# Rows of attention maxima: from TensorE products with the identity to a VectorE block transpose and a trip through DRAM

## The chip, the cores and the metric

The kernel runs on one core of a Trainium2 chip. The metric is the time of one execution on the device in microseconds (us), and the figure quoted for a kernel is the median of several executions. Profiles are single executions with the hardware profiler on. The engines are called as in the profile: PE (TensorE, with PEld for its weight loads), DVE (VectorE), ACT (ScalarE), POOL (GpSimd) and SP (SyncE, which here only issues transfers).

## The reference, cut to what matters

One layer: attention over 4096 tokens of width 256 with 16 heads of width 16, then a residual and a layer norm, then a gated feed-forward part with hidden width 1024, a second residual and a second layer norm. The change lies in the attention:

```python
proj = quant4(x) @ ternary_weight(Wqkv_w).T + Wqkv_b
q = proj.reshape(B, N, h, dk).transpose(0, 2, 1, 3)
k = proj.reshape(B, h, N, dk)
v = proj.reshape(B, h, N, dk)
q, k = (rotary(q, N), rotary(k, N))
ql, kl = (q @ U, k @ U)
att = jnp.einsum('bhnr,bhmr->bhnm', ql, kl) / math.sqrt(dk)
y = jax.nn.softmax(att, axis=-1) @ v
...
return quant4(y) @ ternary_weight(Wo_w).T
```

The softmax needs the largest score of every query and head. The kernel computes all scores twice: once with queries on the partitions, to find the maxima, and once with keys on the partitions, to make the weights, with the maximum subtracted inside the product.

## The kernel before, in words

**Units and steps.** The attention is cut into 64 units (`NU`): 8 pairs of heads times 8 blocks of 512 queries (`QB`). A unit `u` has 32 steps (`NKT`), so there are 2048 steps. Each step of the main loop at line 690 can do three things, all for different places of the stream:

- `largest(s)`: two score products (L463, one for each head `j` of the pair, each over 64 rows) into two PSUM tiles of the pool `ps_1`, which has three buffers, and one DVE reduction to a maximum for each (L471). At the last step of a unit, DVE reduces the 8 partial maxima of each query and head to one (L476), rounds it to the matmul type (L483) and keeps the rest of the rounding as a second part (L484). The two parts go into columns 0, 1 and 64, 65 of `m_aug`, a 128 x 128 tile for each of the four query tiles, otherwise zero.
- `weights(s - LAG)`: four products (L504) into one tile `sc`: first minus ones times the rows of maxima, `mrows[u]`, which starts each sum with the negated maximum, then keys times queries. ACT then takes the exponential of 128 x 1024 values (L512).
- `values`: once in two steps, eight products of the weights with the values (L526) into the tile `av`.

**The rows of maxima.** The maxima come out of `largest` with a query on each partition, and `weights` needs them as rows along the free dimension. `largest_rows(u)` does that: four products of `m_aug` with the identity (L491) into one `ps_1` tile, and an ACT copy of it to `mrow` in SBUF (L495). It is put at step 32(u+1)+2, that is two steps after the unit's last maxima, and the unit's first `weights` follow at step 32u+LAG, with `LAG` = 36, two steps later still.

**Order.** Nothing is scheduled by a planner. `at(step, f)` puts a piece of work at a step; at each step, first that list runs, then `largest` (odd steps) or `weights`, then the other. Every engine takes its instructions in that written order. Apart from the three streams the list holds the making of queries (L426, L434) and keys (L356 to L395), the projection of later blocks of x, the end of a unit (`finish`, L541 to L565, at the steps `base + NKT + AVLAG - 1` and `+ 3`, with `base` = 32u + `LAG`), the comparison of weights with their rounded copies (L582 to L590, one chunk every second unit, its DVE reduction at step 30 of a unit), and weight loads near the end. SP issues the x and weight-check loads (L626, L582) and the writes of a unit's output to `y_dram` (L565), also in written order.

**Start and end.** In steps 0 to 35 only `largest` runs, and after step 2047 only `weights` and `values` run, for `LAG` steps and a few more. Then the feed-forward part follows (`ffn`), PE-bound and untouched by the change; its first block's preparation, `start_front`, is put at the fixed steps 2050 to 2070.

Of the kernel before, what the change touches and what calls it, by code (L numbers as in the profile page):

```python
# [9 lines left out]
F32 = mybir.dt.float32  # L10
F32R = mybir.dt.float32r
# [3 lines left out]
ALU = mybir.AluOpType  # L15
AX = mybir.AxisListType
PSUM = bass.MemoryType.PSUM

P = 128
# [6 lines left out]
QB = 512  # L26
NQB = N // QB
NKT = N // P
DH = 1024
NC = DH // P  # L30
BT = 4
# [6 lines left out]
def attn_ffn_kernel(  # L38
# [22 lines left out]
    nc = tc.nc  # L61
# [4 lines left out]
    stat = ctx.enter_context(tc.tile_pool(name="stat", bufs=4))  # L66
# [6 lines left out]
    identr = const.tile([P, P], F32R, name="identr")  # L73
# [6 lines left out]
    dram = ctx.enter_context(tc.tile_pool(name="dram", bufs=1, space=bass.MemoryType.DRAM))  # L80
# [157 lines left out]
    with ExitStack() as actx:  # L238
        big = actx.enter_context(tc.tile_pool(name="big", bufs=1))
# [11 lines left out]
        gmat = big.tile([P, P], F32, name="gmat")  # L251
        minus = big.tile([P, P], F32R, name="minus")

        m_aug = [big.tile([P, BT, P], F32R, name=f"m_aug{i}") for i in range(2)]

        qpool = actx.enter_context(tc.tile_pool(name="qpool", bufs=2))
        ppool = actx.enter_context(tc.tile_pool(name="ppool", bufs=8))
# [2 lines left out]
        ps_1 = actx.enter_context(tc.tile_pool(name="ps_1", bufs=3, space=PSUM))  # L260

        def bank1(shape, dt):
            return ps_1.tile(shape, dt, name="ps1")

        def set_up():

            nc.sync.dma_start(out=x_bufs[0], in_=x_t[:, ts(0, BT), :])
            tw = [ppool.tile([P, 2, D], F32, name=f"tw{i}", tag="pr") for i in range(2)]
            wabs = ppool.tile([P, 2, 2, D], F32, name="tabs", tag="pr")
            neg = ppool.tile([P, 2, 2, D], F32, name="tneg", tag="pr")  # L270
            nc.sync.dma_start(out=tw[0], in_=wqkvT.rearrange("(k p) o -> p k o", p=P))
            small = ppool.tile([P, 2 * QB], F32, name="small", tag="pr")
            ut, ut8, mask = small[:32, :DK], small[:32, P : 2 * P], small[:, 2 * P : 3 * P]
            nc.sync.dma_start(out=ut, in_=uT)
            nc.sync.dma_start(out=mask, in_=blockmask)
            tables = ((cos, cos_q, cos_k), (sin, sin_q, sin_k))
            for src, _, tk in tables:
                nc.sync.dma_start(out=tk, in_=src.rearrange("(a p c) f -> p a c f", a=2, p=P))
            nc.sync.dma_start(out=bias_bc, in_=bqkv.partition_broadcast(P))
            for src, tq, _ in tables:  # L280
                nc.sync.dma_start(out=tq, in_=src.rearrange("(t p) f -> p t f", p=P))
            nc.sync.dma_start(out=x_bufs[1], in_=x_t[:, ts(1, BT), :])
            nc.sync.dma_start(out=tw[1], in_=woT.rearrange("(k p) o -> p k o", p=P))

            ternary(tw[0], wabs[:, 0], neg[:, 0], bank1, sgn_qkv, alpha_qkv)
            nc.gpsimd.tensor_copy(
                ut8.rearrange("r (j e) -> r j e", e=DK), ut.unsqueeze(1).broadcast_to([32, 8, DK])
            )
            psg = bank1([P, 512], F32)
            nc.tensor.matmul(psg[:, :P], lhsT=ut8, rhs=ut8, start=True, stop=True)  # L290
            nc.vector.tensor_tensor(gmat, psg[:, :P], mask, ALU.mult)

            def later():

                nc.gpsimd.memset(minus.bitcast(F32), -1.0)
                for i in range(2):
                    nc.gpsimd.memset(m_aug[i].bitcast(F32), 0.0)
                nc.gpsimd.memset(v_chunk[:, :, :, DK : DK + 1], 1.0)
                nc.gpsimd.memset(v_all[:, :, H * (DK + 1) :], 0.0)
                ternary(tw[1], wabs[:, 1], neg[:, 1], bank1, sgn_o, alpha_o)  # L300

            return later
# [140 lines left out]
            return natural, transposed  # L443

        NU = (H // 2) * NQB
        LAG = NKT + 4
        AVLAG = 4
        kTs, qTs, mxs, mrows, avs, probs = {}, {}, {}, {}, {}, {}
        todo = {}

        def at(step, f):
            todo.setdefault(step, []).append(f)

        def largest(s):

            u, i = divmod(s, NKT)
            qt, ck = divmod(i, NKT // BT)
            if i == 0:
                mxs[u] = stat.tile([P, BT, 2, NKT // BT], F32, name="mx")
            ps = [ps_1.tile([P, 512], F32, name="ps1") for j in range(2)]  # L460
            for j in range(2):
                rows = slice(64 * j, 64 * j + 64)
                nc.tensor.matmul(  # L463
                    ps[j],
                    lhsT=qTs[u][rows, ts(qt, P)],
                    rhs=kTs[u // NQB][rows, ts(ck, 512)],
                    start=True,
                    stop=True,
                )
            for j in range(2):  # L470
                nc.vector.tensor_reduce(  # L471
                    mxs[u][:, qt, j, ck : ck + 1], ps[j], AX.X, ALU.max
                )
            if i == NKT - 1:
                m = stat.tile([P, BT, 2], F32, name="m")
                nc.vector.tensor_reduce(  # L476
                    m.rearrange("p t j -> p (t j)").unsqueeze(2),
                    mxs.pop(u).rearrange("p t j c -> p (t j) c"),
                    AX.X,
                    ALU.max,  # L480
                )
                parts = m_aug[u % 2].rearrange("p t (j e) -> p t j e", j=2)
                nc.vector.tensor_copy(parts[:, :, :, 0], m)  # L483
                nc.vector.tensor_tensor(  # L484
                    parts[:, :, :, 1], m, parts[:, :, :, 0].bitcast(F32), ALU.subtract
                )

        def largest_rows(u):
            ps = ps_1.tile([P, 512], F32, name="ps1")
            for t in range(BT):  # L490
                nc.tensor.matmul(  # L491
                    ps[:, ts(t, P)], lhsT=m_aug[u % 2][:, t], rhs=identr, start=True, stop=True
                )
            mrows[u] = qpool.tile([P, QB], F32R, name="mrow")
            nc.scalar.copy(mrows[u], ps)  # L495

        def weights(s):

            u, kt = divmod(s, NKT)
            ps = ps_sc.tile([P, 2, QB], F32, name="sc")  # L500
            for first in (True, False):
                for j in range(2):
                    rows = slice(64 * j, 64 * j + 64)
                    nc.tensor.matmul(  # L504
                        ps[:, j, :],
                        lhsT=minus[rows, :] if first else kTs[u // NQB][rows, ts(kt, P)],
                        rhs=mrows[u][rows, :] if first else qTs[u][rows, :],
                        start=first,
                        stop=not first,
                    )  # L510
            pr = ppool.tile([P, 2, QB], F32, name="pr")
            nc.scalar.activation(pr, ps, AF.Exp)  # L512
            probs[s] = pr
# [90 lines left out]
        with tc.manual_schedule():  # L604
# [15 lines left out]
            for b in range(1, NQB):  # L620
                steps = projection_steps(b, nc.gpsimd)
                first = NKT * (b - 2) + 16 if b > 1 else 0
# [13 lines left out]
            for u in range(NU):  # L636
                pair, qb = divmod(u, NQB)
                if qb == 2 and pair + 1 < H // 2:
                    def start_keys(pair=pair, u=u):
                        kTs[pair + 1] = kpool.tile([P, N], F32R, name="kT")  # L640
                        steps = key_steps(pair + 1, kTs[pair + 1])
                        for i, f in enumerate(steps):
                            at(NKT * u + 40 + 6 * i, f)
                    at(NKT * u + 8, start_keys)

                def start_queries(u=u, pair=pair, qb=qb):
                    qTs[u] = qpool.tile([P, QB], F32R, name="qT", bufs=3)
                    natural, transposed = query_steps(pair, qb, qTs[u])
                    natural()
                    at(NKT * (u - 1) + 26 if u else 0, transposed)  # L650

                if u:
                    at(NKT * (u - 1) + (18 if u == 1 else 6), start_queries)
                else:
                    start_queries()
                at(NKT * (u + 1) + 2, lambda u=u: largest_rows(u))
                base = NKT * u + LAG
                for kt in range(0, NKT, 2):
                    at(base + kt + 1 + AVLAG, lambda s=NKT * u + kt: values(s))
                at(base + NKT + AVLAG - 1, lambda u=u: finish(u, 0))  # L660
                at(base + NKT + AVLAG + 3, lambda u=u: finish(u, 1))
# [27 lines left out]
            at(last - 60, start_front)  # L689
            for s in range(NKT * NU + LAG + AVLAG + 6):  # L690
                while todo.get(s):
# [221 lines left out]
```

## Time and profile before

| | |
|---|---|
| time, median of 3 | 3807.73 us (3806.94 to 3809.1) |
| the profiled execution's own time | 3807.1 us |
| its span in the profile | 3805.3 us |
| granted TensorE clock, mean | 0.99 of full speed |
| DVE busy | 3075.3 us, 81% of the span |
| ACT busy | 2383.2 us, 63% |
| POOL busy | 458.5 us, 12% |
| four identity products (L491) per unit | 64 times, 42.8 us busy in all |
| ACT copy of the rows (L495) | 64 times, 37.1 us busy in all |
| first of L491, last of L504 | 99.4 us, 3123.5 us after the start |

The attention takes the first 3130 us or so, the feed-forward part the rest. A line of the profile's groups or timeline reads: line of the source, engine, operation, output tile <- input tiles, shape, count, then busy time; in square brackets stands how long the engine was idle before it and what ended the wait. PE matmuls are pipelined and overlap in the record, so distances between starts say more of PE's pace than the sum of durations.

### The profile page before, as it was taken

Reading aid. Unit: us, or ns where it says so; the run is one execution under the profiler, and the core shown is the slowest. Engines: PE = TensorE matmul, PEld = TensorE weight load, DVE = VectorE, ACT = ScalarE, POOL = GpSimd, SP = SyncE. Lnnn points to the kernel's source line nnn. Section 1 sums busy time; section 2 is a strip of 40 time slices with the busy share of each in tenths; the row PEclk is TensorE's granted clock in tenths of the full one; section 3 lists DMA queues with packets and bytes.
Section 4 is the critical chain, followed back from the end, with each engine's and each line's share of the span. In section 5 each row is a group of like instructions: output and inputs, shape, how many; then the busy total and the mean of one; then the engine's idle time right before and its main releaser. Section 6 shows DMA issues by size and latency. Waiting matters only on the chain.

```text
span 3805.3 us, 61552 instructions
## 1 busy us (share of the span) xinstructions
PE 3732.7 (98%) x24907; PEld 2112.6 (56%) x24907; DVE 3075.3 (81%) x5340; ACT 2383.2 (63%) x2694; POOL 458.5 (12%) x775
## 2 busy tenths in 40 slices
PE   6999999999999999999999999999999999999998
PEld 3445555555555555555555555555555548888887
DVE  6888998899889888898899889988989954555554
ACT  1666777777777777777777777667777773333333
POOL 3242011001100110111001100110010000000000
PEclk7999999999999999999999999999999999999999
DMA  1000000000000000000000000000010010000000
GB/s 41 7 13 3 8 8 8 8 8 8 8 8 8 8 8 8 8 8 8 8 8 8 8 8 8 8 2 13 14 47 13 8 55 21 17 17 22 29 6 13
DMA packets 69110, 49.34 MB, mean 13 GB/s; under 512 B 43984, under 2 KB 63696, under 8 KB 68816
## 3 DMA queue, kind: packets, MB, share of 16 engines
q1 hardware_dynamic: 64992, 33.78, 3.3%
q0 software_dynamic: 3824, 11.54, 0.9%
q8 instruction: 197, 3.23, 0.3%
q14 instruction: 97, 0.79, 0.1%
HBM read 36.92 MB, written 8.39 MB: 12 GB/s over the span
## 4 chain that ended last, share of the span: by engine, by line
PE 93%; DVE 5%; ACT 1%; issue 0%; POOL 0%; DMA 0%; SPq 0%; ACTq 0%; DVEq 0%
PE av L526 26%; PE sc L504 24%; PE ps L463 21%; PE ps_mm L745 17%; DVE mx L471 3%; PE ps L546 1%; PE ps L491 1%; PE ps L388 1%; PE ps L434 1%; DVE differ L590 1%; PE ps L362 0%; ACT pr L512 0%; PE ps L147 0%; PE ps L356 0%; DVE ma L119 0%
## 5 line engine op out<-in xcount | busy, mean ns | idle before, releaser
L471 DVE TENSOR_REDUCE mx<-ps 128x1 f32<-128x512 f32 x4096 | 2560.3, 684 | 320.5 <-PE ps L463 296.6
L512 ACT ACTIVATE pr<-sc 128x1024 f32<-128x1024 f32 x2048 | 2011.9, 1024 | 889.2 <-PE sc L504 884.8
L463 PEld LDWEIGHTS ps<-kT,qT 64*128 64x128 f32 x4096 | 563.7, 185 | 998.5 <-DVE mx L471 643.1
L463 PE MATMUL ps<-kT,qT 64*128 64x512 f32 x4096 | 1081.3, 470 | 18.4 <-DVE mx L471 15.1
L526 PE MATMUL av<-pr,v_all 128*32 128x512 f32 x8192 | 1091.4, 605 | 0.0
L504 PE MATMUL sc<-mrow,minus 64*128 64x512 f32 x4096 | 866.7, 406 | 3.1 <-ACT pr L512 3.0
L504 PE MATMUL sc<-qT,kT 64*128 64x512 f32 x4096 | 833.2, 390 | 0.0
L504 PEld LDWEIGHTS sc<-qT,kT 64*128 64x128 f32 x4096 | 409.2, 185 | 77.6
L504 PEld LDWEIGHTS sc<-mrow,minus 64*128 64x128 f32 x4096 | 402.1, 185 | 75.5 <-ACT pr L512 18.3
L526 PEld LDWEIGHTS av<-pr,v_all 128*32 128x32 f32 x8192 | 161.6, 108 | 263.7 <-issue 262.6
L778 ACT ACTIVATE gate<-ps_mm,sc_hs 128x512 f32<-128x512 f32 x128 | 88.3, 690 | 312.5 <-PE ps_mm L745 269.4
L727 DVE CAST h<-gate 128x512 fp32r<-128x512 f32 x128 | 54.4, 425 | 223.0 <-ACT gate L778 222.9
L586 POOL CAST wround<-xs 128x1024 fp32r<-128x1024 f32 x22 | 22.8, 1038 | 1410.8 <-DMA xs<-in_h1T 505.8
L729 DVE TENSOR_TENSOR h<-gate,h 128x512 fp32r<-128x512 f32 x192 | 132.4, 690 | 5.1
L745 PE MATMUL ps_mm<-h,h1a 128*128 128x512 f32 x512 | 128.9, 394 | 0.0
L745 PE MATMUL ps_mm<-h,h2a 128*128 128x512 f32 x512 | 127.1, 390 | 0.0
L745 PE MATMUL ps_mm<-h,h2b 128*128 128x512 f32 x512 | 126.5, 389 | 0.0
L745 PE MATMUL ps_mm<-h,h1b 128*128 128x512 f32 x512 | 126.5, 389 | 0.0
L770 DVE SCALAR_TENSOR_TENSOR gate<-ps_mm,sc_s,gate 128x512 f32<-128x512 f32 x64 | 48.1, 751 | 81.9 <-ACT gate L768 58.0
L745 PEld LDWEIGHTS ps_mm<-h,h1b 128*128 128x128 f32 x512 | 96.1, 188 | 20.1
L745 PEld LDWEIGHTS ps_mm<-h,h2b 128*128 128x128 f32 x512 | 96.1, 188 | 19.9
L745 PEld LDWEIGHTS ps_mm<-h,h2a 128*128 128x128 f32 x512 | 95.6, 188 | 19.5
(148 smaller groups left out, 1992.6 us busy)
## 6 DMA issues: line engine op xcount, KB each, us to landing
xs<-in_x SPq DMA_DIRECT2D x16, 512.0 KB, 3.9
y_dram<-yu SPq DMA_DIRECT2D x64, 64.0 KB, 1.8
xs<-in_h1T SPq DMA_DIRECT2D x8, 512.0 KB, 3.8
xs<-in_h2T SPq DMA_DIRECT2D x8, 512.0 KB, 3.8
yb<-y_dram SPq DMA_DIRECT2D x8, 512.0 KB, 4.8
out<-xs SPq DMA_DIRECT2D x8, 512.0 KB, 2.9
h1a<-in_h1T POOLq DMA_DIRECT2D x2, 1024.0 KB, 6.2
h1b<-in_h1T POOLq DMA_DIRECT2D x2, 1024.0 KB, 6.9
```

What stands on the lines that cost most here:

```text
L388: nc.tensor.matmul(ps[:, ts(k, P)], lhsT=flat[:, ts(4 * i + k, P)], rhs=identr, start=True, stop=True,)
L434: nc.tensor.matmul(ps[:, ts(t, P)], lhsT=qq[:, t].rearrange("p j k e -> p (j k e)"), rhs=identr, start=True, stop=True,)
L463: nc.tensor.matmul(ps[j], lhsT=qTs[u][rows, ts(qt, P)], rhs=kTs[u // NQB][rows, ts(ck, 512)], start=True, stop=True,)
L471: nc.vector.tensor_reduce(mxs[u][:, qt, j, ck : ck + 1], ps[j], AX.X, ALU.max)
L504: nc.tensor.matmul(ps[:, j, :], lhsT=minus[rows, :] if first else kTs[u // NQB][rows, ts(kt, P)], rhs=mrows[u][rows, :] if first else qTs[ ...
L512: nc.scalar.activation(pr, ps, AF.Exp)
L526: nc.tensor.matmul(avs[u][strip : strip + 32, :], lhsT=v_all[:, 2 * (2 * pair + j) + a, c * (DK + 1) : c * (DK + 1) + 32], rhs=probs[s + k ...
L727: eng(dst[:, k, 0, :], g)
L729: nc.vector.tensor_tensor(dst[:, k, 1, :], g, dst[:, k, 0, :].bitcast(F32), ALU.subtract)
L745: nc.tensor.matmul(ps, lhsT=sb[:, ks, ts(o, P)] if split else wo[:, k, :], rhs=src[:, k, i, :], start=(k == 0 and i == 0), stop=(k == n - ...
L770: nc.vector.scalar_tensor_tensor(g, pb, scales["s2"][:, o : o + 1], gate, ALU.mult, ALU.mult)
L778: nc.scalar.activation(g, ps, AF.Gelu, scale=scales[sc][:, o : o + 1])
```

## The change

The four products with the identity and the ACT copy go. After the unit's last maxima DVE writes the two parts into a small 128 x 32 tile, `m_parts`, whose columns are part, head, kind and query tile (a half of it stays zero). One DVE instruction transposes it in blocks of 32 x 32 into `m_turned`. SP writes that to DRAM (16 KB), and then reads it back with four transfers, each one row of 512 values into one partition (0, 1, 64, 65) of `m_rows`, in runs of 128 bytes. `m_rows` has two buffers, cleared once at the start. `weights` reads `m_rows` instead of `mrows`. `LAG` grows from 36 to 40, so `weights`, `values` and `finish` of every unit run four steps later against `largest` and everything at fixed steps.

```diff
-        m_aug = [big.tile([P, BT, P], F32R, name=f"m_aug{i}") for i in range(2)]
+        m_parts = big.tile([P, 2, 2, 2, BT], F32R, name="m_parts")
+        m_turned = big.tile([P, 32], F32, name="m_turned")
+        m_rows = [big.tile([P, QB], F32R, name=f"m_rows{i}") for i in range(2)]
+        m_dram = [dram.tile([P, 32], F32, name=f"m_dram{i}") for i in range(2)]
...
+                nc.gpsimd.memset(m_parts.bitcast(F32), 0.0)
                 for i in range(2):
-                    nc.gpsimd.memset(m_aug[i].bitcast(F32), 0.0)
+                    nc.gpsimd.memset(m_rows[i].bitcast(F32), 0.0)
...
-        LAG = NKT + 4
+        LAG = NKT + 8
...
-                m = stat.tile([P, BT, 2], F32, name="m")
+                m = stat.tile([P, 2, BT], F32, name="m")
                 nc.vector.tensor_reduce(
-                    m.rearrange("p t j -> p (t j)").unsqueeze(2),
-                    mxs.pop(u).rearrange("p t j c -> p (t j) c"),
-                    AX.X,
-                    ALU.max,
-                )
-                parts = m_aug[u % 2].rearrange("p t (j e) -> p t j e", j=2)
-                nc.vector.tensor_copy(parts[:, :, :, 0], m)
+                    m, mxs.pop(u).rearrange("p t j c -> p j t c"), AX.X, ALU.max
+                )
+                parts = m_parts[:, 0]
+                nc.vector.tensor_copy(parts[:, :, 0, :], m)
                 nc.vector.tensor_tensor(
-                    parts[:, :, :, 1], m, parts[:, :, :, 0].bitcast(F32), ALU.subtract
-                )
-
-        def largest_rows(u):
-            ps = ps_1.tile([P, 512], F32, name="ps1")
-            for t in range(BT):
-                nc.tensor.matmul(
-                    ps[:, ts(t, P)], lhsT=m_aug[u % 2][:, t], rhs=identr, start=True, stop=True
-                )
-            mrows[u] = qpool.tile([P, QB], F32R, name="mrow")
-            nc.scalar.copy(mrows[u], ps)
+                    parts[:, :, 1, :], m, parts[:, :, 0, :].bitcast(F32), ALU.subtract
+                )
+                nc.vector.transpose(
+                    m_turned, m_parts.bitcast(F32).rearrange("p a j k t -> p (a j k t)")
+                )
+
+                turned = m_dram[u % 2]
+                nc.sync.dma_start(out=turned, in_=m_turned)
+                turned = turned.rearrange("(b a j k t) c -> a j k t b c", b=4, a=2, j=2, k=2)
+                for j in range(2):
+                    for k in range(2):
+                        row = m_rows[u % 2][64 * j + k : 64 * j + k + 1, :].bitcast(F32)
+                        nc.sync.dma_start(
+                            out=row.rearrange("o (t b c) -> o t b c", t=BT, b=4),
+                            in_=turned[0, j, k].unsqueeze(0),
+                        )
...
-                        rhs=mrows[u][rows, :] if first else qTs[u][rows, :],
+                        rhs=m_rows[u % 2][rows, :] if first else qTs[u][rows, :],
...
-                at(NKT * (u + 1) + 2, lambda u=u: largest_rows(u))
```

More of the change, by code (lines that the diff above doesn't have):

```diff
@@ L445, in attn_ffn_kernel @@
         NU = (H // 2) * NQB
-        LAG = NKT + 4
+        LAG = NKT + 8
         AVLAG = 4
-        kTs, qTs, mxs, mrows, avs, probs = {}, {}, {}, {}, {}, {}
+        kTs, qTs, mxs, avs, probs = {}, {}, {}, {}, {}
         todo = {}
```

## The prediction

> **What bounds the kernel now.** I read the page first: shares of the engines, then the chain that ended last.
>
> ```profile
> PE 3732.7 (98%) x24907; PEld 2112.6 (56%) x24907; DVE 3075.3 (81%) x5340; ACT 2383.2 (63%) x2694; POOL 458.5 (12%) x775
> PE 93%; DVE 5%; ACT 1%; issue 0%; POOL 0%; DMA 0%; SPq 0%; ACTq 0%; DVEq 0%
> ```
>
> PE carries 93% of the chain and DVE only 5%. By line the chain gives L491, the products to be removed, 1.0% of the span, about 38 us. So PE time saved in the attention is worth nearly its face value, as long as nothing else ends last in its place. Whether that holds is read from one unit. The timeline of PE around the last maxima of a unit, where `values` (L526) marks every second step:
>
> ```profile
> 2045.54 1.06 PE L526 MATMUL av<-pr,v_all 128*32 128x512 f32 x8
> 2046.53 0.50 PE L463 MATMUL ps<-kT,qT 64*128 64x512 f32 x2
> ...
> 2048.25 1.06 PE L526 MATMUL av<-pr,v_all 128*32 128x512 f32 x8
> 2049.24 0.95 PE L463 MATMUL ps<-kT,qT 64*128 64x512 f32 x2
> ...
> 2050.57 0.66 PE L491 MATMUL ps<-identr,m_aug 128*128 128x128 f32 x4
> ...
> 2052.06 1.07 PE L526 MATMUL av<-pr,v_all 128*32 128x512 f32 x8
> ```
>
> The columns are start, length, engine, line. An undisturbed pair of steps takes 2048.25 - 2045.54 = 2.71 us. The pair with the rows of maxima takes 2052.06 - 2048.25 = 3.81 us, so 1.10 us more. It has two parts: the pair of L463 lasts 0.95 instead of 0.50 us (0.45 of waiting), and the rest, 0.65 us, is L491 itself (its piece of the chain is 0.59 us) with the switch into and out of it. The DVE timeline at the same place tells what the 0.45 is:
>
> ```profile
> 2047.07 1.29 DVE L471 TENSOR_REDUCE mx<-ps 128x1 f32<-128x512 f32 x2 [0.23 <-PE ps L463]
> 2048.40 0.22 DVE L476 TENSOR_REDUCE m<-mx 128x8 f32<-128x64 f32 x1
> 2048.65 0.17 DVE L483 CAST m_aug<-m 128x8 fp32r<-128x8 f32 x1
> 2048.86 0.17 DVE L484 TENSOR_TENSOR m_aug<-m,m_aug 128x8 fp32r<-128x8 f32 x1
> 2048.95 2.48 DVE L471 TENSOR_REDUCE mx<-ps 128x1 f32<-128x512 f32 x4
> 2052.16 3.91 DVE L471 TENSOR_REDUCE mx<-ps 128x1 f32<-128x512 f32 x6 [0.74 <-PE ps L463]
> ```
>
> Four reductions take 2.48 us, so DVE has only 0.23 us of slack in a pair of steps. The three small operations on `m` hold it up for 0.55 us (2048.40 to 2048.95). The second L463 of the next step needs the `ps_1` buffer that the reduction from 2048.95 frees at about 2049.6, and PE stands until then. This stall is DVE's and stays. Behind it DVE is idle for 0.74 us, because PE is in L491: DVE does not bound the rest.
>
> **The change part by part.**
>
> *L491 and L495 go.* PE gets 0.65 us back in each unit: 64 x 0.65 = 41.6 us. It falls on the path wherever PE is the bound, which the first 36 steps and the end hardly change (2 of 64 units). The ACT copy (0.58 us, 64 times) frees ACT time off the path: ACT waits 0.75 us or so in each pair of steps there, so it is costed at nothing. L491's buffer in `ps_1` goes too. After the stall the following L463 need the buffers of reductions at 0.62 us intervals, and PE comes to them after 0.93 us of L504: just enough room (DVE's 0.74 us of idleness shrinks to about 0.1), so no new stall is put in the sum.
>
> *The DVE transpose.* It stands in the same row of small operations, between L484 and the next L471, so its time lengthens the 0.45 us stall one for one. The trace has no transpose on DVE. Its nearest rows are the 128x8 cast (175 ns, 0.21 from start to start) and the 128x64 reduction (220 ns); 32 columns lie between. I take 0.21 us: 64 x 0.21 = 13.4 us. The low end is 0.05 us, if it overlaps the next reduction as L484 does; the high end 0.45, twice the reduction, if it drains DVE on both sides. Below nothing is excluded, an instruction is added. The Trainium skill ("VectorE: DVE Perf Modes", The three transpose paths) gives a 128x128 bf16 transpose 311 ns on VectorE and 390 ns on TensorE, so by it the move gains little; our operation has a quarter of the columns, and TensorE's place here cost 0.65. With 0.31 for 0.21 the sum would lose 64 x 0.10 = 6.4 us, 3790 instead of 3783.5. I go by the rows, since at these sizes their length hardly moves with the columns (175 to 220 ns from 8 to 64). The other three DVE operations keep their element counts: nothing.
>
> *The trip.* SP issues five transfers for each unit. What the trace shows of such transfers:
>
> ```profile
> y_dram<-yu SPq DMA_DIRECT2D x64, 64.0 KB, 1.8
> sc_s<-in_s SPq DMA_DIRECT2D x2, 4.0 KB, 1.7
> 415.14 0.99 SPq L633 DMA_DIRECT2D sc_s<-in_s  x2
> ```
>
> A store of 64 KB in 128-byte runs lands 1.8 us after issue; a small load takes 1.7 (the 1 KB one 1.9); each issue holds SP for about 0.5 us (0.99 for two). So the trip is 1.8 + 0.1 for the wait + 3 x 0.5 for the first three loads + 1.9 for the fourth = 5.3 us. The Trainium skill ("DMA: Bandwidth & Descriptors", Specifications and Anatomy of one DMA) speaks against it: under 512 B a transfer pays a read-modify-write, and each transfer has about 2.0 us of fixed cost, HBM writes the worst. The row with just such runs says 1.8; by the page's fixed cost the trip is an estimated 5.6 us and the sum is the same, because of the room: the transpose ends near 2048.86 + 0.42 = 2049.3, and step 33's L463 stands at 2049.24. `weights` of step 40 comes three pairs (8.1 us), the stalls (0.7) and L463 with one half of L504 (0.8) later, 2058.8. The window is 9.5 us, 4.2 more than the trip. On SP's queue, the `y_dram` write now lies at step 15 of a unit's period (from 11) with `LAG` shifting `finish` from 7 to 11 for its DVE part, loads for the weight check at 14, x loads at 28: all issued by step 31, and none waits on something later than that (the long waits of L565 are SP having nothing to do; the one x load that waited for POOL was issued by 75.2 us, the first maxima end at 97). What now queues behind a waiting `m` write is only the next unit's output or load, tens of us early. POOL gets one more small memset at the start. The trip is costed at nothing; uncovered, each us costs 63 us.
>
> *Lag 36 to 40.* Four steps of all three streams (1.353 each) become four of `largest` alone (DVE: 1.24) at the start and four of `weights` and `values` at the end. The chain at the end:
>
> ```profile
> 3114.64 1.13 PE sc L504 x7
> 3115.76 1.00 PE av L526 x8
> 3116.76 1.37 PE sc L504 x8
> 3118.13 1.00 PE av L526 x8
> ```
>
> Four steps take 4.5 us there, 1.12 each. So the lag costs 4 x (1.24 + 1.12 - 1.353) = 4.0 us; between 2 (if the end's steps go at ACT's 1.0 and the start hides some) and 6. The shifted `finish` meets other work of the list at other steps; the same work, costed at nothing, plus or minus 2.
>
> *Sum:* -41.6 + 13.4 + 4.0 = -24.2 us against the profiled execution's 3807.1 us, 3782.9. The median of the runs is 0.6 above that execution: 3783.5.
>
> **The rivals.**
>
> *The trip doesn't fit (slower).* PE would stand at the first L504 of every unit. The place is that wait, and it decides from a trip of 9.5 + 24.2/63 = 9.9 us on. For it: two transfers in sequence with SP between them, and loads in this trace that landed late (a 2 KB load at the start took 4.4 us behind others, one store 10.0). With 4.4 for both legs the trip is 4.4 + 0.1 + 1.5 + 4.4 = 10.4 us, 0.9 uncovered: 63 x 0.9 = 57, 3840 us. Against it: those were loads behind 512 KB of others, and in steady state the DMA engines are idle at 0.1 busy or less. 8%.
>
> *DVE swallows half of it.* The transpose costs 0.45, or the next L463 finds its buffer late because L491's pause no longer lets DVE catch up (0.3 a unit). Either adds 15 to 19 us: 3799 to 3803. For it: DVE's slack of 0.23 in a pair of steps, and the 22 units with a 1.2 us reduction (L590) just before. 18%.
>
> *More gain.* The transpose overlaps (0.05) and the list collides less: 3783.5 - 10 - 2 = about 3772. 9%.
>
> *It does nothing.* That PE's 0.65 is filled by another wait altogether needs DVE at its limit over the unit; with 442 us busy in 500 it isn't. 4%.
>
> **How the numbers follow.** My forecast (3775 to 3796) has 61%. Faster by over 0.2% (about what a measurement of this kernel can tell from no change, here 7.6 us, below 3800.1) takes it, the greater gain and two thirds of the DVE rival: 0.82. Within 0.2%: the rest of that rival and half of the case of nothing: 0.08. Slower: the trip, and the other half, where the lag's 4 us and the transpose are left uncovered: 0.10. The range reaches from the greater gain to just past the DVE rival: 3772 to 3804.
>
> **What would show it right or wrong.** L491 and L495 gone; the transpose near 0.2 us in DVE's list; the pair of steps after a unit's last maxima at about 2.71 + 0.66 = 3.4 us instead of 3.81, its L463 near 1.15; the last row landing about 5.3 us after the transpose, and no idle time before the first L504 of a unit; the last L504 about 24 us earlier, near 3099. I am wrong if PE waits for a DMA there, if the transpose is over 0.5 us, or if a second stall of L463 follows the first.

## The result, and the profile after

The changed kernel takes 3778.03 us (median of 6, 3776.26 to 3779.2) against 3808.08 us before (6 runs): a ratio of 0.992, 95% interval 0.9907 to 0.9933. In a later set of runs it took 3777.94 against 3809.4, 0.9919 (0.9905 to 0.9932). So it is 30 to 31 us faster by the medians; forecast were 24 us faster, 3783.5, range 3772 to 3804. Its profiled execution took 3776.26 us with a span of 3774.5. The engines and the chain of the changed kernel:

```profile
PE 3693.2 (98%) x24651; PEld 2084.5 (55%) x24651; DVE 3081.1 (82%) x5404; ACT 2351.2 (62%) x2630; POOL 458.9 (12%) x776
PE 89%; DVE 10%; issue 1%; ACT 0%; POOL 0%; DMA 0%; SPq 0%; ACTq 0%; DVEq 0%
```

PE lost 256 products, ACT 64 copies, DVE gained 64 transposes. DVE's share of the chain doubled, from 5 to 10%: with the products away, the chain now goes through DVE's small operations behind each unit's last maxima. DMA has no share, and in this profile nobody waits for the rows. The lines moved: L463 is now L468, L471 is L476, L504 is L511, L526 is L533.

The timeline of PE at the same place as shown of before, the pair of steps after a unit's last maxima:

```profile
2025.38 1.07 PE L533 MATMUL av<-pr,v_all 128*32 128x512 f32 x8
2026.38 0.50 PE L468 MATMUL ps<-kT,qT 64*128 64x512 f32 x1
2027.03 0.50 PE L468 MATMUL ps<-kT,qT 64*128 64x512 f32 x1 [0.16 <-DVE mx L476]
...
2028.66 1.06 PE L533 MATMUL av<-pr,v_all 128*32 128x512 f32 x8
```

The pair of steps takes 3.28 us, where it took 3.81, and 0.57 us more than an undisturbed pair of 2.71; this surplus is called the excess of a pair below. It is now the wait of the second L468 for its PSUM buffer, which DVE frees: in an undisturbed pair the two L468 start together, here the second starts 0.65 us after the first, and 0.57 of it is left at the next L533. DVE at that time:

```profile
2024.20 1.29 DVE L476 TENSOR_REDUCE mx<-ps 128x1 f32<-128x512 f32 x2 [0.21 <-PE ps L468]
2025.53 0.22 DVE L481 TENSOR_REDUCE m<-mx 128x8 f32<-128x64 f32 x1
2025.79 0.17 DVE L485 CAST m_parts<-m 128x8 fp32r<-128x8 f32 x1
2025.99 0.17 DVE L486 TENSOR_TENSOR m_parts<-m,m_parts 128x8 fp32r<-128x8 f32 x1
2026.19 0.21 DVE L489 STREAM_TRANSPOSE m_turned<-m_parts 128x32 f32<-128x32 f32 x1
2026.33 3.64 DVE L476 TENSOR_REDUCE mx<-ps 128x1 f32<-128x512 f32 x6
```

From 2025.53 to 2026.33 DVE is away from its reductions for 0.80 us; before it was 0.55. The pair's 0.57 us are this lump of small operations less DVE's slack (its idle time in an undisturbed pair) of 0.23 us. And SP's issues for the same unit:

```profile
2026.43 0.32 SPq L494 DMA_DIRECT2D m_dram<-m_turned  x1
2027.91 2.65 SPq L499 DMA_DIRECT2D m_rows<-m_dram  x4
```

The store to DRAM goes out 0.03 us after the transpose, its landing lets the first load out after 1.48 us, and the four loads hold SP 0.66 us each. At the end of the attention the chain has not changed its pace: four steps take 4.5 us as before.

```profile
3085.86 1.37 PE sc L511 x8
3087.24 1.00 PE av L533 x8
3088.23 1.13 PE sc L511 x8
3089.36 1.00 PE av L533 x8
```

The last L511 starts at 3093.0 us, about 31 us earlier than the last L504 of before (3123.9), and the feed-forward part is as long as it was: all of the gain lies in the attention.

### The profile page after: what moved, and what is told of

The parts are those of the page before. It is cut to its first block, busy times and chain, and to the rows that moved or that the text cites. A ratio compares the mean times of both kernels' runs of the same rounds, so it can differ in the third digit from the quotient of the medians.

```text
span 3774.5 us, 61722 instructions
## 1 busy us (share of the span) xinstructions
PE 3693.2 (98%) x24651; PEld 2084.5 (55%) x24651; DVE 3081.1 (82%) x5404; ACT 2351.2 (62%) x2630; POOL 458.9 (12%) x776
## 4 chain that ended last, share of the span: by engine, by line
PE 89%; DVE 10%; issue 1%; ACT 0%; POOL 0%; DMA 0%; SPq 0%; ACTq 0%; DVEq 0%
PE av L533 25%; PE sc L511 22%; PE ps L468 20%; PE ps_mm L751 17%; DVE mx L476 7%; PE ps L553 1%; PE ps L393 1%; PE ps L439 1%; DVE differ L597 1%; PE ps L367 0%; DVE m L481 0%; DVE m_turned L489 0%; DVE m_parts L485 0%; DVE m_parts L486 0%; PE ps L361 0%
## 5 line engine op out<-in xcount | busy, mean ns | idle before, releaser
L476 DVE TENSOR_REDUCE mx<-ps 128x1 f32<-128x512 f32 x4096 | 2552.0, 683 | 279.6 <-PE ps L468 261.0
L468 PEld LDWEIGHTS ps<-kT,qT 64*128 64x128 f32 x4096 | 574.0, 185 | 1020.2 <-DVE mx L476 707.3
L468 PE MATMUL ps<-kT,qT 64*128 64x512 f32 x4096 | 1101.2, 471 | 27.4 <-DVE mx L476 23.1
L533 PE MATMUL av<-pr,v_all 128*32 128x512 f32 x8192 | 1091.4, 605 | 0.0
L511 PE MATMUL sc<-m_rows,minus 64*128 64x512 f32 x4096 | 865.0, 403 | 3.1 <-ACT pr L519 3.0
L511 PE MATMUL sc<-qT,kT 64*128 64x512 f32 x4096 | 836.1, 390 | 0.0
L511 PEld LDWEIGHTS sc<-qT,kT 64*128 64x128 f32 x4096 | 418.6, 185 | 80.2
L511 PEld LDWEIGHTS sc<-m_rows,minus 64*128 64x128 f32 x4096 | 412.3, 185 | 75.8 <-ACT pr L519 22.8
L533 PEld LDWEIGHTS av<-pr,v_all 128*32 128x32 f32 x8192 | 161.6, 108 | 258.6 <-issue 257.5
L431 POOL CAST qq<-qn 128x256 fp32r<-128x256 f32 x64 | 25.5, 398 | 739.2 <-PE ps L439 737.1
```

The lines of the kernel that those rows point to most:

```text
L468: nc.tensor.matmul(ps[j], lhsT=qTs[u][rows, ts(qt, P)], rhs=kTs[u // NQB][rows, ts(ck, 512)], start=True, stop=True,)
L476: nc.vector.tensor_reduce(mxs[u][:, qt, j, ck : ck + 1], ps[j], AX.X, ALU.max)
L511: nc.tensor.matmul(ps[:, j, :], lhsT=minus[rows, :] if first else kTs[u // NQB][rows, ts(kt, P)], rhs=m_rows[u % 2][rows, :] if first else ...
L533: nc.tensor.matmul(avs[u][strip : strip + 32, :], lhsT=v_all[:, 2 * (2 * pair + j) + a, c * (DK + 1) : c * (DK + 1) + 32], rhs=probs[s + k ...
```

## The experiments

**The lag alone.** One edit to the kernel before:

```diff
-        LAG = NKT + 4
+        LAG = NKT + 8
```

> The kernel before with LAG 40 and nothing else (products with the identity kept). Theory A, the lag is a plain cost at both ends: four steps of maxima alone are gained at the start and four of weights and values alone paid at the end. My sum says +4.0 us (3812); read from the first and last instructions of the two traces it is -1.4 at the start and +4.5 at the end, +3.1 (3811). Rival B: the 5.5 us by which the change beat the prediction comes from the end of a unit (finish) meeting other work of the step list at better steps; then the lag alone is worth -1 us or better (3807 or less).

Measured: 3815.93 us against 3810.07 for the kernel before on the same chip, ratio 1.0015 (1.0008 to 1.0022): +5.9 us. Rival B falls: the lag is a cost. By the median it is also above both sums of theory A, but the interval, 3.0 to 8.4 us, takes them in. The profile of this run ends 8.9 us after that of before, in three parts. The first `values` come 4.8 us later, about as four DVE-bound steps of 1.24 should. Within the stream 2.5 us are added: six units have a pair of 1.62 to 1.68 us excess after their maxima where before had 1.12, 3 us together, and small gains elsewhere offset part. From the first `values` of the last unit to the end it loses 1.5 us more, where PE runs for some us at a lower clock. The windows of this run (columns: us, busy time of PE, PEld, DVE, ACT, POOL with instructions, granted clock, DMA share, GB/s):

```profile
3105.00:3110.00 5.00, 2.40 (x20) 0.76 (x16) 1.56 (x5) 4.56 (x5) 0.00 (x0) 0.95 0.02 3
3110.00:3118.00 8.00, 7.59 (x40) 2.78 (x44) 0.00 (x0) 4.57 (x6) 0.00 (x0) 0.61 0.00 0
```

PE stands 3 us there, while ACT loads function tables twice (1.28 us each), and then has 0.61 of its clock on average over 8 us. In the profiles of before and of the changed kernel it stands as long and keeps its clock. The kernel before has no profile from this set of runs, where it took 2 us more than in the first, so I take the timed 5.9 us for the lag and leave its parts open.

**The products alone.** To the kernel before, without changing the lag:

```diff
+        m_none = big.tile([P, QB], F32R, name="m_none")
...
-                        rhs=mrows[u][rows, :] if first else qTs[u][rows, :],
+                        rhs=m_none[rows, :] if first else qTs[u][rows, :],
...
-                at(NKT * (u + 1) + 2, lambda u=u: largest_rows(u))
```

> The kernel before (LAG 36) without the four products with the identity and the ACT copy; the rows of maxima are a constant tile, so the maxima are found but not subtracted. The DVE work stays. It measures what the removed part was worth. By the prediction's split (0.65 us a unit, 64 units) -41.6 us: 3766. By theory C, that the 1.10 us a unit were 0.32 us of DVE stall (0.55 us of small operations less 0.23 of slack) and 0.78 us for the products, -50 us: 3758.

Measured: 3762.61 against 3810.07, ratio 0.9875 (0.986 to 0.989): -47.5 us. The interval runs from -53 to -42 us; the prediction's 41.6 lies at its edge, theory C's 50 inside. The pair of steps decides between them. PE's timeline after the maxima:

```profile
2019.07 1.07 PE L528 MATMUL av<-pr,v_all 128*32 128x512 f32 x8
2022.12 1.06 PE L528 MATMUL av<-pr,v_all 128*32 128x512 f32 x8
```

It takes 3.05 us, 0.35 of excess. So of before's excess of 1.12 us (1.10 in the unit that the prediction shows) 0.77 were the products, and 0.35 the three small DVE operations: the prediction's split of 0.65 and 0.45 falls, theory C's 0.78 and 0.32 nearly holds. In most units the products were worth this much, 0.66 in one of eight. Over 62 units the pairs sum to 46.5 us. Between the two profiles it is 45.7 us at the first `values` of the last unit, and 44.4 at the end of the attention, since this run, too, loses clock there. All three agree with the timed 47.5 within its interval.

**The transpose twice.** To the changed kernel:

```diff
+                nc.vector.transpose(
+                    m_again, m_parts.bitcast(F32).rearrange("p a j k t -> p (a j k t)")
+                )
                 nc.vector.transpose(
                     m_turned, m_parts.bitcast(F32).rearrange("p a j k t -> p (a j k t)")
                 )
```

> The changed kernel with the DVE transpose done twice (the first into a tile nobody reads). It measures one more DVE operation in the same place. By theory C every such operation lengthens the stall by its start-to-start time, 0.2 to 0.25 us in 62 units: +13 to +16 us, 3791 to 3794. By the split that the result suggests if the products were worth 0.65 (0.53 gained a unit, so the transpose costs 0.12), +7 to +8 us: 3786. If DVE had room for it, under +3.

Measured: 3780.37 against 3810.07, ratio 0.9923 (0.991 to 0.9937). Set against the changed kernel's 0.992 and 0.9919 that is about one us, within the intervals: only the expected "under +3" fits, so the +13 to +16 that I had drawn from theory C was wrong. The DVE timeline tells why:

```profile
2026.81 0.21 DVE L490 STREAM_TRANSPOSE m_again<-m_parts 128x32 f32<-128x32 f32 x1
2026.95 0.17 DVE L493 STREAM_TRANSPOSE m_turned<-m_parts 128x32 f32<-128x32 f32 x1
2027.04 3.64 DVE L477 TENSOR_REDUCE mx<-ps 128x1 f32<-128x512 f32 x6
```

The second transpose doesn't need the first, so it starts 0.14 us behind it, and the reduction 0.09 behind that: the lump grew by 0.09 us only (2026.15 to 2027.04, 0.89), not by 0.2. The pair's excess grew by the same 0.09, from 0.57 to 0.66: lump less 0.23 again. (Over 62 units the pairs sum to 5 us, and the profile is 3 us longer; about one us was timed, and the intervals are too wide to tell these apart.) My expectation took the start-to-start time of a chain of dependent operations for an independent one. On the price of the transpose in the change this run says nothing; that stands in the pair: 0.57 - 0.35 = 0.22 us in most units, 0.03 in the one of eight where key work covers it, 12.1 us over 62 units.

**The trip with less lag.** The changed kernel with one edit, in two versions. First `LAG` back at 36:

```diff
-        LAG = NKT + 8
+        LAG = NKT + 4
```

> The changed kernel with LAG back at 36: the trip is left a window of 4.1 us (from the end of the transpose to the first L504 of the unit, 9.5 less two pairs of 2.7). If the trip takes the 5.3 us of the prediction, PE waits 1.2 us in each of 63 units, 76 us, less 5 for the lag: 3849. If the rows land in 4 us or less, there is no wait and the lag's 5 to 6 us come back: 3773. A wait here that is not DVE's measures the trip.

Measured: 3861.47 us against 3809.4, ratio 1.0135 (1.012 to 1.0151), 83.5 us over the changed kernel on the same chip. PE's timeline in one unit:

```profile
1217.19 0.39 PE L511 MATMUL sc<-qT,kT 64*128 64x512 f32 x2
1218.47 0.46 PE L511 MATMUL sc<-m_rows,minus 64*128 64x512 f32 x1 [0.90 <-DMA m_rows<-m_dram]
1219.81 0.46 PE L511 MATMUL sc<-m_rows,minus 64*128 64x512 f32 x1 [0.87 <-DMA m_rows<-m_dram]
...
1220.67 1.32 PE L533 MATMUL av<-pr,v_all 128*32 128x512 f32 x8
```

PE stands first for the rows of one head, then of the other. In more than half of the units the pair's excess is 1.30 to 1.58 us, so with the window of 4.1 us the trip takes 5.4 to 5.7. In the unit shown the first transfer took 2.47 us instead of 1.47:

```profile
1213.40 0.33 SPq L494 DMA_DIRECT2D m_dram<-m_turned  x1
1215.87 2.64 SPq L499 DMA_DIRECT2D m_rows<-m_dram  x4
```

Its pair has 2.34 us of excess and the next one 1.40, since the clock falls after the waits (windows, columns as above):

```profile
1219.00:1221.00 2.00, 1.19 (x9) 0.67 (x13) 0.42 (x1) 0.40 (x1) 0.00 (x0) 1.00 0.01 1
1221.00:1223.00 2.00, 2.00 (x14) 0.89 (x8) 1.12 (x3) 0.62 (x1) 0.00 (x0) 0.59 0.04 8
1223.00:1226.00 3.00, 3.00 (x20) 1.32 (x18) 2.15 (x4) 2.02 (x3) 0.00 (x0) 0.71 0.00 0
```

Seven units, six of them with a first transfer of 2.1 to 2.7 us, lose 2 to 4 us each, 23 us together. With them the loss comes to 83 us instead of the 71 that the expectation worked out. With `LAG = NKT + 6`, 38:

> The changed kernel with LAG 38: window 6.8 us. If the trip is 5.3 us it fits and half of the lag's cost comes back: 3775 (-3). If the trip is over 6.8, PE waits the rest in each unit: 3778 + 63 us for every us over.

Measured: 3776.1 against 3809.4, 0.9911 (0.9896 to 0.9926), with no PE wait for a DMA in its profile. Beside it ran the changed kernel:

> The changed kernel once more, beside the next three on one chip, so that they can be set against it within one per mille: 30 us under the kernel before.

3777.94. The trip fits in 6.8 us, as expected of 5.4. The 2 us that two steps of lag should bring are the difference of the medians, but the intervals overlap. In the profile the first `values` do come 1.9 us earlier, but at the end of the attention the clock fell, and 3.1 us were lost.

**The small operations spread.** In the changed kernel the four DVE operations become functions, put apart by the step list:

```diff
+                for n, f in enumerate((overall, high, low, turn)):
+                    at(s + 2 + 2 * n, f)
...
-        LAG = NKT + 8
+        LAG = NKT + 14
```

Here `overall` is the reduction to `m`, `high` the cast, `low` the subtraction, and `turn` the transpose with its five transfers.

> The changed kernel with the four small DVE operations at the end of a unit set apart, one in every second step (steps 33, 35, 37, 39 of the unit instead of all after step 31), the transfers behind the last of them, and LAG 46 to leave room for them. If the stall is the lump of 0.80 us against a slack of 0.23 us in each pair of steps, each operation now fits its pair: the 0.57 us a unit go (62 x 0.57 = 35), the six steps of lag cost 6 x 0.8 = 5: 3778 - 30 = 3748. If the slack can't take an operation of 0.2 us (PE and DVE in lock step), nothing is gained and the lag shows: 3783.

Measured: 3753.11 against 3810.07, ratio 0.985 (0.9835 to 0.9865), the fastest of all by its median; 57 us under the kernel before in the same set of runs, and about 26 under the changed kernel, where 30 were expected. DVE's and then PE's timeline:

```profile
2008.84 0.21 DVE L484 TENSOR_REDUCE m<-mx 128x8 f32<-128x64 f32 x1
2009.14 2.48 DVE L476 TENSOR_REDUCE mx<-ps 128x1 f32<-128x512 f32 x4
2011.55 0.16 DVE L489 CAST m_parts<-m 128x8 fp32r<-128x8 f32 x1
...
2014.25 0.16 DVE L492 TENSOR_TENSOR m_parts<-m,m_parts 128x8 fp32r<-128x8 f32 x1
...
2016.96 0.20 DVE L497 STREAM_TRANSPOSE m_turned<-m_parts 128x32 f32<-128x32 f32 x1
```

```profile
2010.32 1.06 PE L543 MATMUL av<-pr,v_all 128*32 128x512 f32 x8
2013.03 1.07 PE L543 MATMUL av<-pr,v_all 128*32 128x512 f32 x8
2015.73 1.07 PE L543 MATMUL av<-pr,v_all 128*32 128x512 f32 x8
2018.44 1.07 PE L543 MATMUL av<-pr,v_all 128*32 128x512 f32 x8
```

Each operation stands where DVE was idle, just before the reductions of the next odd step, and every pair shown is back at 2.71 us. The same four operations cost 0.57 us in a lump and nothing apart. That is the strongest evidence for theory C. (In the profiles the stream gains 30.7 us between the first `values` and those of the last unit, against the 35 expected; but the six steps of lag start it 9.1 us later.) Two steps of lag less:

> The version with the four DVE operations spread, with LAG 44 for 46. The trip starts at step 39 and has a window of 6.2 us, measured need 5.4: two steps of lag come back, 2 us under the spread version (ratio to the kernel before 0.9845 or so). If transfers are delayed in some units as in the version with POOL, up to 10 us over it.

Measured: 3756.04 against 3809.05, 0.9861 (0.9844 to 0.9877). No gain over LAG 46. In the profile the first `values` come 3.3 us earlier than at LAG 46, and most of it is lost again in three units late in the stream, where the first transfer took 2.7 to 3.6 us. The waits for the rows, PE and its weight load counted apart:

```profile
  DMA m_rows<-m_dram: 6.0, 9
```

The window, 6.2 us by the expectation and 5.8 in most units of the profile, leaves too little over a trip that is now and then slower.

**The rounding on POOL.** From the spread version, the cast and the subtraction go to POOL right behind the reduction, and the transpose comes two pairs later, with LAG 42:

```diff
-                        nc.vector.tensor_copy(parts[:, :, 0, :], m)
+                        nc.gpsimd.tensor_copy(parts[:, :, 0, :], m)
...
-                for n, f in enumerate((overall, high, low, turn)):
-                    at(s + 2 + 2 * n, f)
+                for n, f in ((2, overall), (2, high), (2, low), (6, turn)):
+                    at(s + n, f)
```

> The kernel with the small operations spread (no lump on DVE), with the rounding and the rest of it on POOL instead of DVE (reduction at step 33 on DVE, the two on POOL behind it, the transpose at step 37 on DVE) and LAG 42 in place of 46. If the lump was all of the stall, DVE has only two operations of 0.2 us in slacks of 0.23 and it keeps the gain of the spread version, 27 us, and gets back 4 steps of lag, 3 to 4 us: 3748. If POOL, busy with queries and keys, hands the parts over late, DVE waits at the transpose and the reductions behind it: over 3753.

Measured: 3777.35 against 3809.4, 0.9915 (0.9902 to 0.9929): all of the spread version's gain is gone. Neither of the two outcomes that I described fits: DVE has no wait at its transposes. In the profiles this version ends 22 us after the spread one, and 20 of them lie in three units near the end. POOL's and SP's timelines in one of the three:

```profile
2766.61 1.49 POOL L171 DMA_DIRECT2D h1a<-in_h1T  x2
```

```profile
2768.33 0.34 SPq L501 DMA_DIRECT2D m_dram<-m_turned  x1
2775.96 2.63 SPq L506 DMA_DIRECT2D m_rows<-m_dram  x4
```

The first transfer, 1.5 us elsewhere, takes 7.6 us here, and 5.6 and 6.3 in the other two; in all three POOL had issued 1.5 to 2 MB of weights in the 2 us ahead of it. The suspicion: POOL had nothing to wait for between handing over the unit's parts and the load, so it issued the load at once, ahead of the step in whose list it stands. In the spread version, without POOL's wait, the same load goes out at 2720.70 us, between two trips. To test it, a tiny POOL copy of a fresh maximum was put ahead of each of these loads, and the second w2 load moved by six steps (`hold` makes the copy):

```diff
+            for d in (240, 230, 214, 180, 140):
+                at(last - d, lambda d=d: hold(last - d))
```

> The version with the rounding on POOL and LAG 42, with one tiny POOL copy of a fresh DVE maximum put ahead of each weight load of the attention (and the second w2 load at step 1834 for 1828), so that POOL, which in that version ran ahead to the load as soon as it had handed over a unit's parts, issues each load at the step it was written for. Theory: in that version four weight loads were issued within 2 us of the start of a trip and stretched its first transfer from 1.5 to 5.6-7.6 us, about 20 us of PE waits. Then 3777 - 20 = 3757 or less, 3750 if nothing else differs from the spread version. If the loads were not the cause, 3777 stays.

Measured: 3756.74 against 3809.05, 0.9864 (0.9848 to 0.988). The same unit:

```profile
2769.47 0.19 POOL L684 COPY held<-mx 128x1 f32<-128x1 f32 x1 [12.37 <-DVE mx L476]
2769.71 1.49 POOL L171 DMA_DIRECT2D h1a<-in_h1T  x2
```

```profile
2758.77 0.34 SPq L501 DMA_DIRECT2D m_dram<-m_turned  x1
2762.10 2.63 SPq L506 DMA_DIRECT2D m_rows<-m_dram  x4
```

The load now follows the rows, and about 20 us are back: the loads were the cause. The first transfer still took 3.3 us in this unit; the cause of that stays open. There is no lead over LAG 46 on DVE alone, so the simple spread version stays the best. What four steps less of lag give back at the start (5.9 us in the profile, 6.2 with the loads not held) both POOL versions lose again by the sixth unit: their first five units take 258 and 260 us against 250. Why is not shown.

## Why the prediction was right, point by point

- *L491 and L495 go:* 41.6 us forecast, 47.5 timed alone, 46.5 by the pairs. The mechanism was right, the term was 5 to 6 us small. The step that was off is the split of 1.10 us into 0.45 of stall and 0.65 of products. I read the stall off the length of the L463 record; by the lump less the slack, 0.55 - 0.23 = 0.32, it was smaller, and without the products it measured 0.35. Both numbers stood in the lines shown.
- *The transpose:* 0.21 us forecast, 212 ns long and 0.22 of stall in most units; 13.4 us in the sum, 12.1 by the pairs, since in one of eight units key work covered it. Going by the nearest rows held against the 311 ns of the Trainium skill (VectorE: DVE Perf Modes, The three transpose paths), which are for a wider operation in another type.
- *The trip:* 5.3 us forecast, 5.4 to 5.7 found with the lag back at 36, and its place and price as in the slower rival: at that lag the rival is what happens. That the sum came out so close is in part luck, since the parts were off against each other: the first leg 1.48 us instead of 1.9 with the wait, the issues 0.66 us instead of 0.5. The first leg also stayed under the page's 2.0 us of fixed cost, which it fits to transfers issued by GpSimd. Whether the read-modify-write below 512 B that the Trainium skill speaks of (DMA: Bandwidth & Descriptors, Specifications) cost anything, no run here shows: none sets the runs of 128 bytes against longer ones.
- *The lag:* 4.0 us forecast, 5.9 measured alone (3.0 to 8.4), at the upper end of its bounds.
- *The sum:* -47.5 + 12.1 + 5.9 = -29.5 us from the measured parts, -30.05 and -31.5 measured. So close an agreement is luck, as the first term alone is known to 5 or 6 us, and the lag was measured beside the products: its six slower pairs, 3 us, do not come back in the changed kernel. The forecast's -24.2 is off by the products above all.
- *The rivals:* DVE did not swallow the gain (no second stall followed the first); it did become the cause of all that is left of the place, and the spread version takes that too. The result lies inside the forecast's own 3775 to 3796, not at the 3772 of the greater gain, and what that rival rested on did not come: the transpose did not hide.
- *The signs:* the pair of 3.28 us (3.4 forecast), the second L468 ending 1.15 us after the first starts (1.15), and no PE wait for a DMA came as named.

## What to carry to other kernels

Where two engines ran nearly in step, as PE and DVE here, the price of extra work on the faster one was the lump less its slack, once (lumps of 0.55, 0.80 and 0.89 us less 0.23 against 0.35, 0.57 and 0.66 measured); the same work in pieces of the size of the slack, one for each turn, cost nothing. The round trip through DRAM of 5.4 us was free with the consumer 9.5 us behind, and the margin had to cover the slow units, not the typical one. And an engine that takes its instructions in order issues a transfer when its last wait ends, not at the step where it was written: with POOL's added wait, the weight loads met the trip, and 20 us were lost.

## What was not expected of the hardware

Single-partition loads of 2 KB in runs of 128 B held SP's issue for 0.60 to 0.66 us each, where the 128-partition store of 16 KB took 0.32. PE's clock fell to 0.59 and 0.71 (means of the windows) after waits of 0.90 and 0.87 us in a row (LAG 36). After the wait of 2 to 3 us near the end of the attention it stayed at 1.00 in before, in both profiles of the changed kernel and in the POOL version, and fell in the other eight. The 7 us behind that wait in the changed kernel and in its version with LAG 38:

```profile
3073.00:3080.00 7.00, 6.97 (x52) 2.63 (x52) 0.00 (x0) 5.77 (x6) 0.00 (x0) 1.00 0.00 0
3074.30:3081.30 7.00, 7.00 (x34) 2.60 (x36) 0.00 (x0) 3.80 (x4) 0.00 (x0) 0.59 0.00 0
```

What decides it is not shown. It can cost a run 1 to 3 us, as much as some of the differences above. And a transpose behind another that it does not need starts 0.14 us after it, against 0.20 to 0.26 in a dependent chain.
